# A state-space convolution block: stores, seeds and statistics reordered, the first gates computed in the head

## The chip, the cores and the metric

The kernel runs on one core of a Trainium2 chip. The metric is device time in microseconds (us), as the median of the runs shown. Engines are named as in the profile: PE (TensorE matmul), PEld (its weight loads), DVE (VectorE), ACT (ScalarE), POOL (GpSimd) and SP (SyncE, which issues nearly all DMAs here).

## What is computed

The input is `x` of 4 images, 128 channels, 96 x 96. It is normalised in 32 groups of channels, laid out as four sequences (rows forward and reversed, columns forward and reversed), put through one block with shared weights, and the four results are fused and added to `x`:

```python
def _scan1d(x, ...):                       # HID, MH, G, K = 256, 32, 4, 5
    t = _grouped1x1(x, in_proj_w, in_proj_b, G)
    u, gate = (t[:, :HID], t[:, HID:])
    u = silu(u)
    u = depthwise_conv(u, dw_w)            # 5 taps along the sequence
    s = _conv1x1(u, ssm_in_w)
    a = DMIN + (DMAX - DMIN) * sigmoid(_conv1x1(u, ssm_delta_w, ssm_delta_b))
    bb = tanh(_conv1x1(u, ssm_b_w, ssm_b_b))
    cc = tanh(_conv1x1(u, ssm_c_w, ssm_c_b))
    hst = <first-order recurrence h = a * h + bb * s along the sequence>
    u = u + _conv1x1(cc * hst + ssm_d[None, :, None] * s, ssm_out_w)
    u = _grouped1x1(u * sigmoid(gate), mix_w, mix_b, G)
    return _conv1x1(u, out_proj_w, out_proj_b)
...
return x + fuse(concat of the four directions)
```

## The kernel before

**Units, pairs, phases.** The work is cut into 8 phases: for each of the 4 images first the column order ("V"), then the row order ("H"). A phase has 6 steps of 4 pairs, so 24 pairs (`NP`), and there are 192 pairs in all. A pair `t` has two units `s` = 0 and 1, a forward and a reversed sequence, each of 384 positions with 256 channels in two halves `j`. A step's four pairs have the places `p` = 1, 2, 3, 0 (`TURN`); "offset" below is `t % 24`, and `k = t % 4`.

**Front and back.** In pair `t` the front works 4 pairs ahead: `front(t + 4)` does the input projection and SiLU of a quarter of a step (`compute_front`). Only steps 0 to 2 of a phase compute it ("fresh"); steps 3 to 5 are the same data met from the other end and load the SiLU stored before. A pair with a computed front is called fronted (offsets 20 to 23 and 0 to 7), the others unfronted. The pair's own convolution follows: half `j` = 1 by five taps on VectorE (`taps`, L765, the first tap on ScalarE, L763), half `j` = 0 by band matmuls on PE (`conv`). What the band lacks at the edge comes in two ways: places `p` = 1 and 2 add "less" matmuls (`conv_less`, which ends with a ScalarE copy of `u` out of PSUM, L736 or L738), places 3 and 0 ("single" pairs) add a row block on VectorE (`add_lone`, L717), from a tile that `keep_lone` stores to DRAM and `load_lone` brings back. `proj` computes `s`, `a`, `bb`, `cc` (PE, then ScalarE L802, L805, L810, then GpSimd L812, L813). `recurrence` runs the scan on VectorE (L839) in pairs with `k` < 2 and the outputs on GpSimd (L845 to L848). `scale_s` (L822) is the multiplication by `ssm_d`.

The back works `LAG` = 6 pairs behind, on pair `n = t - 6`: `under` (L560, ScalarE) seeds two PSUM banks with `u`, `out_of` (L548, PE) adds the state's output, `gating` (L664, VectorE) multiplies by the gate, and one pair later `accumulate` (PE, ScalarE L872 or L874, GpSimd L891) adds the mixed and fused product to the output held in SBUF.

**Gates.** The gate of pair `n` is four matmuls (`gate`, L528) and a tanh on ScalarE (L564, L570). The first 12 gates of a phase are computed, stored in DRAM (`kept`), and the second 12 load one of those, because they meet the same positions from the other end: `mirror(n)` gives offsets 12, 13, 14, 15 the gates 9, 8, 11, 10, and so on. There are two tiles for gates, `tile_of(n) = gates[n % 2]`. The gate of pair `n + 1` is computed in pair `n`; the gates of a phase's first three pairs are computed in pairs of offset 17 to 19, into the tile `shared`, and go through DRAM.

**Order.** `manual_schedule` takes each engine's order, SP's too, from the order in which the code issues. Waits follow from which tile or bank an instruction reads and writes. An instruction that waits holds all that stand behind it on its engine.

**Statistics.** While an image's V phase runs, the next image's input passes through three buffers, and VectorE takes `bn_stats` of 384 columns at a time (`stats_chunks`). In the H phase `stats_finish`, a generator, turns these into weights and biases, two steps of it in every pair with `k` > 1.

**Head.** Pairs 0 to 7 are issued by `pair`, the others by `pair_on`. Pairs 0 to 5 have no back. Pairs 6 and 7 have one, with their own gates computed in place; pair 8 computes two sets of gates (L1084 to L1095 and that of pair 9's `n`).

## Time and profile before

| | us |
|---|---|
| runs of before: median | 1783.57 |
| lowest, highest of 3 | 1782.19, 1784.2 |
| the profiled execution | 1788.7 |
| its span | 1787.0 |
| granted TensorE clock in it | 0.997 |

| group of instructions | count | busy us | mean ns |
|---|---|---|---|
| L765 DVE taps into PSUM | 576 | 589.0 | 1023 |
| L135 PE projection | 6144 | 538.2 | 491 |
| L135 PE mix and fuse | 6192 | 543.1 | 485 |
| L891 POOL add to the output | 375 | 411.2 | 1119 |
| L560 ACT seed | 380 | 298.2 | 799 |
| L738 and L736 ACT copy of u | 53 and 94 | 42.4 and 40.5 | 799 and 483 |
| L822 ACT scaling of s | 192 | 118.4 | 617 |

How to read it: the busy share of an engine is over the whole span; a group is one line of the code with one shape; a row of the timeline has its start, its duration, engine, line, operation, output and input, count, and in brackets the idle time ahead of it with what ended that. Matmuls overlap, four column groups at a time, so a mean duration of PE is no cost of one. PE works through its queue in order, and so do the other engines.

### The profile page before, as it was taken

The page shows a single profiled execution, that of the slowest core. Times are in us where ns is not written, and L with a number is a line of the kernel's source. Part 1 is how long each engine was busy: PE and PEld are TensorE (multiplying, and loading weights), DVE is VectorE, ACT ScalarE, POOL GpSimd, SP SyncE. Part 2 cuts the span into 40 slices and gives each one's busy share as a digit, 9 for nine tenths or more (in the row PEclk, how much of TensorE's full clock was granted, in tenths as well). Part 3 has the DMA queues.
Part 4 walks back from the last instruction along what each step waited for, and adds up shares of the span by engine and source line. Part 5 has one row for each costly group of instructions (what it writes and reads, how often), then busy time and mean ns, then how long its engine had stood idle before and what let it go on. Part 6 is the DMA issues. An engine that isn't in the chain of part 4 may idle for free.

```text
span 1787.0 us, 54377 instructions
## 1 busy us (share of the span) xinstructions
PE 1739.9 (97%) x22618; PEld 661.0 (37%) x22618; DVE 1496.9 (84%) x1526; ACT 1492.7 (84%) x2551; POOL 1423.3 (80%) x1477
## 2 busy tenths in 40 slices
PE   6999999999999999999999999999999999999998
PEld 3334333443334433344333443334433343334433
DVE  6888888887889888888778988888877888888887
ACT  4888888888888888888888888888888888888875
POOL 3578788877878878887777888888787888888886
PEclk9999999999999999999999999999999999999999
DMA  7775975558996688456798688744889749756464
GB/s 238 213 248 193 304 232 166 202 189 278 292 335 233 233 261 243 143 198 230 249 329 301 217 276 262 225 160 163 276 257 316 260 151 311 239 183 198 166 208 176
DMA packets 193814, 417.89 MB, mean 234 GB/s; under 512 B 17312, under 2 KB 154912, under 8 KB 193568
## 3 DMA queue, kind: packets, MB, share of 16 engines
q1 hardware_dynamic: 193424, 414.37, 70.5%
q8 instruction: 179, 2.93, 0.7%
q14 instruction: 67, 0.55, 0.1%
q10 hardware_dynamic: 144, 0.04, 0.0%
HBM read 250.58 MB, written 163.76 MB: 232 GB/s over the span
## 4 chain that ended last, share of the span: by engine, by line
PE 81%; DMA 8%; ACT 4%; DVE 3%; POOL 2%; issue 1%; SPq 1%; DVEq 0%; ACTq 0%; POOLq 0%
PE psum L135 68%; PE psum L548 8%; PE psum L528 5%; DMA kept<-shared 2%; DVE psum L765 1%; DMA x_in<-in_xs 1%; DMA out<-acc 1%; DMA lone<-edge 1%; ACT sil L498 1%; DMA edge<-sil 1%; ACT psum L560 1%; DVE u L664 1%; DMA xs<-in_xr 1%; ACT psum L763 1%; ACT shared L564 0%
## 5 line engine op out<-in xcount | busy, mean ns | idle before, releaser
L765 DVE SCALAR_TENSOR_TENSOR psum<-sil,small,psum 128x768 f32<-128x768 f32 x576 | 589.0, 1023 | 51.7 <-ACT psum L763 26.3
L135 PE MATMUL psum<-u,main 128*32 128x384 f32 x6144 | 538.2, 491 | 13.8 <-ACT shared L564 7.2
L135 PE MATMUL psum<-u,w_fin 128*32 128x384 f32 (+1 forms) x6192 | 543.1, 485 | 1.6 <-ACT ys L872 0.4
L664 DVE SCALAR_TENSOR_TENSOR u<-gate,psum 128x768 f32<-128x768 f32 x376 | 341.8, 950 | 181.2 <-PE psum L548 65.8
L891 POOL TENSOR_TENSOR acc<-ys,acc 128x384 f32<-128x384 f32 x375 | 411.2, 1119 | 21.2 <-ACT ys L874 4.5
L845 POOL TENSOR_TENSOR t<-t,t 64x384 f32<-64x384 f32 (+1 forms) x192 | 235.3, 1225 | 137.8 <-DVE t L839 84.3
L135 PEld LDWEIGHTS psum<-u,w_fin 128*32 128x32 f32 x6192 | 194.5, 110 | 313.0 <-issue 233.9
L135 PEld LDWEIGHTS psum<-u,main 128*32 128x32 f32 x6144 | 181.4, 110 | 342.6 <-issue 219.6
L560 ACT COPY psum<-u 128x768 f32<-128x768 f32 x380 | 298.2, 799 | 9.2 <-DVE u L664 4.4
L135 PE MATMUL psum<-sil,band 128*32 128x384 f32 x3072 | 285.5, 488 | 0.3 <-ACT gate L570 0.3
L846 POOL TENSOR_TENSOR t<-t,t 64x384 f32<-64x384 f32 (+1 forms) x192 | 272.3, 1418 | 15.1
L812 POOL TENSOR_SCALAR t<-tm 64x384 f32<-64x384 f32 x191 | 177.1, 927 | 110.3 <-ACT tm L802 84.0
L763 ACT ACTIVATE psum<-sil,small 128x768 f32<-128x768 f32 x191 | 172.5, 903 | 86.0 <-DVE u L664 83.6
L548 PE MATMUL psum<-t,main 32*128 32x384 f32 x1536 | 209.6, 524 | 4.5 <-ACT psum L560 3.3
L813 POOL TENSOR_TENSOR t<-t,tm 64x384 f32<-64x384 f32 x192 | 196.7, 1025 | 16.8 <-ACT t L805 1.6
L765 DVE SCALAR_TENSOR_TENSOR u<-sil,small,psum 128x768 f32<-128x768 f32 x192 | 194.9, 1015 | 6.9
L498 ACT ACTIVATE sil<-psum,bnorm 128x385 f32<-128x385 f32 x384 | 192.2, 584 | 3.9 <-PE psum L135 1.8
L528 PE MATMUL psum<-x_in,wn 32*128 32x384 f32 x768 | 167.9, 495 | 3.6 <-DVE shift L259 1.4
L135 PEld LDWEIGHTS psum<-sil,band 128*32 128x32 f32 x3072 | 89.8, 108 | 171.3 <-issue 60.6
L874 ACT COPY ys<-psum 128x384 f32<-128x384 f32 x281 | 129.5, 477 | 14.9 <-PE psum L135 11.8
L564 ACT ACTIVATE gate<-psum,bnorm 128x384 f32<-128x384 f32 x148 | 85.8, 581 | 57.1 <-PE psum L528 56.8
L802 ACT ACTIVATE tm<-psum,small 128x384 f32<-128x384 f32 x192 | 111.1, 579 | 11.6 <-PE psum L135 3.4
(105 smaller groups left out, 1512.0 us busy)
## 6 DMA issues: line engine op xcount, KB each, us to landing
sil<-sil SPq DMA_DIRECT2D x128, 770.0 KB, 6.5
gate<-kept SPq DMA_DIRECT2D x113, 768.0 KB, 6.2
kept<-gate SPq DMA_DIRECT2D x75, 768.0 KB, 3.6
lone<-edge SPq DMA_DIRECT2D x46, 770.0 KB, 7.3
x_in<-in_xs SPq DMA_DIRECT2D x194, 96.2 KB, 3.9
edge<-sil SPq DMA_DIRECT2D x96, 192.5 KB, 6.9
out<-acc SPq DMA_DIRECT2D x48, 384.0 KB, 7.9
kept<-shared SPq DMA_DIRECT2D x21, 768.0 KB, 5.2
```

What stands on the lines that cost most here:

```text
L135: nc.tensor.matmul(o[r, : rhs.shape[-1]], lhsT, rhs, start=start, stop=stop, skip_group_check=True)
L498: nc.scalar.activation(sils[step][:, s, j, g, :], bank(bk)[:, : N + 1], AF.Silu, bias=bn[:, 1:2] if j else bn[:, 4 + g : 5 + g],)
L528: nc.tensor.matmul(bank(to)[:, :N], stats[un["b"]][0][r, s, :], x_in[s][r, q, off : off + N], start=True, stop=True)
L548: nc.tensor.matmul(bank(ssm(bi, s) + j)[:, :N], w_so[r, bass.ts(j, P)], z[r, :], start=bi not in seeded, stop=True, skip_group_check=True)
L560: nc.scalar.copy(psum[:, ssm(bi, s) : ssm(bi, s) + 2, :N], us[bi][:, s])
L664: nc.vector.scalar_tensor_tensor(v, g, 1.0, pz, ALU.add, ALU.mult)
L763: nc.scalar.activation(part, src, AF.Copy, scale=w_tap[:, 0:1])
L765: nc.vector.scalar_tensor_tensor(us[i][:, :, 1, :] if k == K - 1 else part, src, w_tap[:, k : k + 1], part, ALU.mult, ALU.add,)
L813: nc.gpsimd.tensor_mul(ta[0:64, p, :], tb[0:64, :], tm[0:64, :])
L845: engine.tensor_mul(ta[0:64, p, r], tb[64:P, r], ta[64:P, p, r])
L846: engine.tensor_add(tb[0:64, r], ta[0:64, p, r], tb[0:64, r])
L891: adder.tensor_add(part, y, part)
```

## The change

It has seven parts.

1. **Head.** `pair` is used for pairs 0 to 5 only. In them VectorE copies `u` out of PSUM (two copies of 128 x 384) where ScalarE did, and GpSimd scales `s`. Each of these pairs also computes one unit of the gates of `n` = 0, 1, 2: two `gate` matmuls into banks 2 and 3, two tanh, a `load_gate`, and a store after the second unit; gates 0 and 1 also stay in their tiles, gate 2 goes through `shared`. Pairs 6, 7 and 8 become ordinary pairs of `pair_on`, without gates in 6 and 7, and pair 8 with one set.
2. **Seed.** In unfronted pairs that are not single, ScalarE's copy of `u` is issued behind `under(bi, 0)`.
3. **Gate tiles.** `tile_of` swaps the two tiles from each phase's middle on. Gates 10 and 11 of a phase aren't stored, and the pairs of offset 14 and 15 don't load one: they read what their tile holds, which is what pairs 12 and 13 loaded. The load for pair 12 is issued in pair 10 and goes to the tile in which the gate of pair 11 was computed.
4. **Edge rows.** `keep_lone` is issued in `after_front` as soon as the fourth quarter of a step has its SiLU; `load_lone` always in the step's first pair.
5. **Order on SP.** At a pair's end the chunk loads and the x loads for later gates are issued ahead of the gate store, no longer behind it.
6. **Statistics.** The generator becomes a table of small functions, each with an offset and one of three places in the pair; four small operations and the scaling of the weights move from VectorE to GpSimd. `stats_chunks` comes behind gating in pairs that are not single.
7. **Scaling at the turn.** At offset 19 `scale_s` is left out at the pair's end and done in pair 20, with that pair's own.

```diff
+    def stats_finish(b):
...
+        def spreads():
+            nc.vector.tensor_copy(mean, pm[:, 0:1])
+            nc.gpsimd.tensor_sub(dev, mv[:, 0:1], mean)
+            nc.gpsimd.tensor_mul(ex, dev, dev)
+            nc.gpsimd.tensor_add(ex, ex, mv[:, 1:2])
+            nc.gpsimd.tensor_scalar(gm4, gmask, mean, None, ALU.mult)
...
+        def guess():
+            bits = inv.bitcast(I32)
+            nc.vector.tensor_single_scalar(bits, var.bitcast(I32), 1, ALU.logical_shift_right)
+            nc.vector.tensor_scalar(bits, bits, -1.0, float(0x5F3759DF), ALU.mult, ALU.add)
+            newton()
...
+        def biases():
+            product(pm[:, 0:4], wn, gm4)
             for g in range(4):
                 for q in range(R):
+                    mm(pm[:, 4 + g : 5 + g], q, wn[0:32, 32 * g : 32 * g + 32], mean[0:32, :], True, True)
...
+        return {
+            (0, 0): gather,
+            (1, 1): means,
+            (1, 2): spreads,
+            (2, 1): variances,
+            (2, 2): lambda: nc.vector.tensor_scalar_add(var, pm[:, 0:2], GN_EPS),
+            (3, 0): guess,
+            (4, 0): newton,
+            (5, 0): newton,
+            (6, 0): scale_w,
+            (7, 1): biases,
+            (7, 2): finish,
+        }
...
+        if g == R - 1 and fresh(step):
+            keep_lone(step)
...
     def tile_of(n):
-        return gates[n % 2]
+        return gates[(n + (n + NP // 2) // NP) % 2]
+
+    def stays(m):
+        return NP // 2 - 3 < m < NP // 2
 
     def load_kept(n):
         m = mirror(n)
-        if n % NP < 3 and NP <= n < NU // 2:
+        if n % NP < 3 and 1 < n < NU // 2:
             nc.sync.dma_start(tile_of(n), kept[n // NP % 2][n % NP])
-        if n < NU // 2 - R and m is not None:
+        if n < NU // 2 - R and m is not None and not stays(m):
             nc.sync.dma_start(tile_of(n), kept[n // NP % 2][m])
...
     def pair(t):
...
+        i = 2 * t
+        banks = head_banks(t)
+        if t == R:
+            load_lone(1)
         if t:
             new_u(i)
             taps(i, range(1, K))
             conv(i, banks)
+            conv_less(i, banks, False)
+            for s in range(2):
+                nc.vector.tensor_copy(us[i][:, s, 0, :], bank(min(banks) + s)[:, :N])
             first_tap(i + 2)
             front(t + R, FRONT if banks == PROJ else (5, 4, 2, 3))
         recurrence(t)
         stats_chunks(t)
...
+        if t == 2:
+            keep_lone(0)
+        load_chunks(t + 2)
+        proj(i, banks)
+        n, s = divmod(t, 2)
+        if s == 0:
+            early[0] = tile_of(n) if n < 2 else shared()[:, : 4 * N].rearrange(
+                "p (s j n) -> p s j n", s=2, j=2
+            )
+        for j in range(2):
+            gate(2 * n, s, j, 2 + j)
+        for j in range(2):
+            tanh_one(n, early[0], s, j, 2 + j)
+        load_gate(2 * n + s + UB)
+        if s:
+            nc.sync.dma_start(kept[0][n], early[0])
+        if t > 0:
+            s = tbs[i - 2][0:64, :]
+            nc.gpsimd.tensor_scalar(s, s, d_sb[0:64, 0:1], None, ALU.mult)
 
     def pair_on(t):
...
-        if k == (1 if fresh(un["step"]) else 0):
+        if k == 0:
             load_lone(un["step"])
...
         if not fronted:
             if not single:
-                conv_less(i, banks)
+                conv_less(i, banks, False)
             under(bi, 0)
...
+            if not single:
+                copy_u(i, banks)
+        add_next(w[1])
         if fronted:
             if not single:
                 conv_less(i, banks)
+            if t % NP == 20:
+                scale_s(i - 4)
             scale_s(i - 2)
...
+        piece(t, 2)
+        if not single:
+            stats_chunks(t)
         first_tap(i + 2)
         if gated is not None:
             tanh_both(gated, to, 0, 6)
-            nc.sync.dma_start(kept[gated // NP % 2][gated % NP], to)
...
+        if t + 2 < end:
+            load_chunks(t + 2)
+        if gated is not None:
             for s in range(2):
                 load_gate(2 * gated + s + UB)
...
+        if gated is not None and not stays(gated % NP):
+            nc.sync.dma_start(kept[gated // NP % 2][gated % NP], to)
...
-        if not fronted:
+        if not fronted and (t % NP != 19 or t + R >= end):
             scale_s(i - 2)
...
         start()
-        for t in range(LAG + 2):
+        for t in range(LAG):
             pair(t)
-        for t in range(LAG + 2, NU // 2):
+        for t in range(LAG, NU // 2):
             pair_on(t)
         tail()
```

More of the change, by code (lines that the diff above doesn't have):

```diff
@@ L733, in conv_less, with copy_u @@
                    False, True)
+        if copy:
+            copy_u(i, banks)
+    def copy_u(i, banks):
+        b0 = min(banks)
         if banks == PROJ:
@@ L896, in accumulate, with piece @@
         return add
-    later, soon = [], []
+    later, soon = {}, []
+    def piece(t, place):
+        later.pop((t % NP, place), lambda: None)()
     waiting, held = [], []
@@ L958, in pair @@
         recurrence(t)
-        un = units[i]
         stats_chunks(t)
-        if t % R == 2 and t < LAG + 2:
-            keep_lone(un["step"])
-        ending = old and t % (2 * NP) > NP + NP // 2
-        def stats_piece(at_end=False):
-            if later and k > 1 and at_end == ending and t % (2 * NP) not in (27, 39):
-                next(later[0], None)
-        if not ahead:
-            free[0] = w[1]
-            stats_piece()
-        if seed and with_front:
-            for s in (1, 0):
-                under(bi, s)
@@ L976, in pair @@
-        for add in held:
-            add()
-        held.clear()
-        if waiting:
-            add = accumulate(waiting.pop(0), w[0], *final)
-            if late:
-                held.append(add)
-            else:
-                add()
-        between = ahead and not old
-        if between:
-            conv_less(i, banks)
-        if seed and not with_front:
-            under(bi, 0)
-        if ahead:
-            accumulate(waiting.pop(0), w[1], *final)()
-            free[0] = w[0]
-            stats_piece()
-            if not between:
-                conv_less(i, banks)
```

261 lines of the change are left out of this document (54 added, 207 removed).

## The prediction

> **What bounds the kernel now.** I read the page first, then the waits, then each engine's timeline for single pairs. The page's first part:
>
> ```profile
> PE 1739.9 (97%) x22618; PEld 661.0 (37%) x22618; DVE 1496.9 (84%) x1526; ACT 1492.7 (84%) x2551; POOL 1423.3 (80%) x1477
> ```
>
> TensorE is busy 97% of the span, so only what PE itself executes or waits for can move the end. The change leaves PE's matmuls almost as they are; the question is where PE stands still or runs slower than its rhythm. One `tm` activation (L802) runs per pair, so the distance of two of them on ScalarE is the length of a pair. ScalarE's timeline (start, duration):
>
> ```profile
> 38.52 0.58 ACT L802 ACTIVATE tm<-psum,small 128x384 f32<-128x384 f32 x1
> ...
> 69.95 0.59 ACT L802 ACTIVATE tm<-psum,small 128x384 f32<-128x384 f32 x1
> ...
> 103.25 0.58 ACT L802 ACTIVATE tm<-psum,small 128x384 f32<-128x384 f32 x1
> ...
> 112.67 0.58 ACT L802 ACTIVATE tm<-psum,small 128x384 f32<-128x384 f32 x1
> ...
> 1130.02 0.58 ACT L802 ACTIVATE tm<-psum,small 128x384 f32<-128x384 f32 x1
> ...
> 1138.55 0.58 ACT L802 ACTIVATE tm<-psum,small 128x384 f32<-128x384 f32 x1
> ...
> 1149.56 0.56 ACT L802 ACTIVATE tm<-psum,small 128x384 f32<-128x384 f32 x1
> ```
>
> Pairs 1 to 5 take 31.4 us together and pairs 6 to 8 take 33.3; pair 9 takes 9.42, pair 122 takes 8.53, and pair 123, which differs from 122 in nothing but a piece of statistics, 11.01. Pairs of one kind repeat to a hundredth except where something is late. The waits that reach PE (engine and line, released by, total us, times, longest):
>
> ```profile
> DVE u L717 <- DMA lone<-edge: 5.6, 2, 3.0
> ...
> ACT shared L564 <- DMA kept<-shared: 10.8, 8, 3.1
> ...
> PE psum L135 <- ACT shared L564: 7.2, 9, 2.6
> ...
> PE psum L135 <- DVE u L717: 4.2, 3, 1.8
> ```
>
> A late edge transfer and a late store of gates each stop PE a few times. These, the statistics, the head, and one short wait in every second unfronted pair are what the change touches.
>
> **The change, part by part.** I give each part as what it does to PE; minus is time saved.
>
> *Seed ahead of the u copy.* In an unfronted pair that is not single (offsets 8, 9, 12, 13, 16, 17 of each 24), ScalarE copies `u` (L738) and then seeds the output banks (`under`, L560). Pair 37 is such a pair, pair 10 is a single one, without that copy:
>
> ```profile
> 361.00 0.58 ACT L872 ACTIVATE ys<-psum,b_fin 128x384 f32<-128x384 f32 x1 [0.17 <-PE psum L135]
> 361.84 0.80 ACT L738 COPY u<-psum 128x768 f32<-128x768 f32 x1 [0.26 <-PE psum L135]
> 362.54 0.81 ACT L560 COPY psum<-u 128x768 f32<-128x768 f32 x1
> ...
> 363.09 0.58 PE L528 MATMUL psum<-x_in,wn 32*128 32x384 f32 x1
> 363.49 0.60 PE L548 MATMUL psum<-t,main 32*128 32x384 f32 x3
> ...
> 117.01 0.58 PE L528 MATMUL psum<-x_in,wn 32*128 32x384 f32 x1
> 117.18 0.60 PE L548 MATMUL psum<-t,main 32*128 32x384 f32 x3
> ```
>
> The first output product comes 0.40 after the gate's product here and 0.17 in the single pair; the seed ends at 363.35, just ahead of 363.49. Seeding first, it would start at 361.6 (after `ys`) and end at 362.4, before PE gets there. That is 0.23 a pair, in 6 x 8 pairs less pair 8, which I count in the head: 47. I take 0.2, **-9.4**; bounds 0 and -10.8. The copy of `u` then ends at 363.2, where the seed ends now; its readers are the projection at the pair's end, and bank 7's gate, which stands behind three output products. If that cover is gone, the saving goes with it.
>
> *Statistics.* PE's, VectorE's and ScalarE's timelines in pair 27 (the same pair as 123, two images earlier), and the same operation in the head:
>
> ```profile
> 271.82 0.24 PE L135 MATMUL psum<-mv,gmean 128*32 128x1 f32 x8 [0.31 <-ACT ys L874]
> ...
> 272.93 1.26 DVE L202 SCALAR_TENSOR_TENSOR ex<-dev,mv 128x1 f32<-128x1 f32 x1
> 274.11 1.25 DVE L204 TENSOR_SCALAR gm<-gmask,mean 128x4 f32<-128x4 f32 x1
> ...
> 276.25 0.91 ACT L763 ACTIVATE psum<-sil,small 128x768 f32<-128x768 f32 x1 [3.60 <-DVE u L664]
> ...
> 20.82 0.22 DVE L202 SCALAR_TENSOR_TENSOR ex<-dev,mv 128x1 f32<-128x1 f32 x1
> ```
>
> Two one-column operations of 1.25 stand in VectorE's row ahead of gating, ScalarE's next tap waits 3.60, and the pair is 11.01 - 8.53 = 2.5 too long. After the change `dev`, `ex` and `gm4` run on GpSimd, whose adds and outputs have a pair's slack, and the rest comes behind gating. Three images: -7.5. Added: the bias product is 40 short matmuls instead of 16, at 0.24/8 = 0.03 each 0.7 a time, +2.1. Sum **-5.4**; bounds -7.5 and 0 (the wait only moves).
>
> Why is the same operation 0.22 in the head and 1.26 here? GpSimd is idle there and adding here. [...]
>
> *Edge rows.* `keep_lone` moves one pair earlier, behind the last SiLU of its step, and `load_lone` from the step's second pair to its first: same four stores and one load, 9 us earlier. On SP they now stand behind the x loads and ahead of reloads, chunks and kept gates; SP may wait for the edge stores there, but nothing behind it is due in that pair. The waits above (PE 4.2, DVE 5.6) go: **-5**; bounds 0 and -5.6.
>
> *Gate stores.* Two stores and two loads of 768 KB fall away per phase (gates 10 and 11; pairs 14 and 15), the others are issued behind the chunk and x loads. The stalls at offsets 18 and 19 come from stores on a full queue (SP's timeline; then engines' busy time, clock, DMA share and GB/s in one 2 us stretch):
>
> ```profile
> 191.90 0.34 SPq L1143 DMA_DIRECT2D kept<-shared  x1
> 192.34 2.09 SPq L299 DMA_DIRECT2D x_in<-in_xs  x2
> ...
> 184.00:186.00 2.00, 2.00 (x28) 0.78 (x24) 1.93 (x3) 1.94 (x4) 1.87 (x2) 1.00 1.09 402
> ```
>
> Gone transfers empty the queue by 768 KB at 402 GB/s, some 2 us each, ahead of these stores; but the store now stands behind up to 2.09 us of issuing. I take half of PE's 7.2: **-3.5**; bounds -7.2 and +7 (1 us at each of seven phases).
>
> *Scaling at the turn.* At offset 19 `scale_s` leaves the place ahead of the next pair's SiLUs:
>
> ```profile
> 204.75 0.62 ACT L822 ACTIVATE t<-t,small 64x384 f32<-64x384 f32 x1
> 205.39 2.00 ACT L498 ACTIVATE sil<-psum,bnorm 128x385 f32<-128x385 f32 x4
> ```
>
> The accumulation waits for those SiLUs' banks, so up to 0.62 in seven phases; 0.5 each, **-3.5**, bounds 0 and -4.3. It is made up for in pair 20 behind the u copies, where ScalarE waits for gating anyway.
>
> *The head.* VectorE's row in pair 4, its chunk wait in pair 2, a PSUM operand of 384 columns on VectorE, and eight gate matmuls:
>
> ```profile
> 60.78 1.75 DVE L839 TENSOR_TENSOR_SCAN t<-t 64x768 f32<-64x768 f32 x1
> 62.57 0.56 DVE L412 BATCH_NORM_STATS2 bn<-xs 128x6 f32<-128x384 f32 x1
> 63.05 3.12 DVE L765 SCALAR_TENSOR_TENSOR psum<-sil,small,psum 128x768 f32<-128x768 f32 x3
> 66.20 1.01 DVE L765 SCALAR_TENSOR_TENSOR u<-sil,small,psum 128x768 f32<-128x768 f32 x1
> ...
> 50.08 0.56 DVE L412 BATCH_NORM_STATS2 bn<-xs 128x6 f32<-128x384 f32 x1 [2.98 <-DMA xs<-in_xr]
> ...
> L891 DVE TENSOR_TENSOR acc<-psum,acc 128x384 f32<-128x384 f32 x5 | 2.7, 545 | 0.0
> ...
> 74.64 1.50 PE L528 MATMUL psum<-x_in,wn 32*128 32x384 f32 x8
> ```
>
> The copy of `u` from PSUM on VectorE isn't in the trace; the nearest row is the add of 545 ns. It could be hidden (0) or held by GpSimd like L202 (1 us more each, ten copies, +10). I take 0.55. VectorE in pairs 1 to 5 then has five times 4.13 of taps and 1.1 of copies, 0.56 in four pairs, a scan in two: 32. The chunk wait keeps its end, so the copies of pairs 1 and 2 fill 2.2 of its 2.98; 0.8 stays, and pair 1 is led by PE, about 1 more: 33.8 against 31.4, **+2.4**. ScalarE loses copies and scaling and gets two tanh; PE gets two gates a pair (0.4), hidden while VectorE leads. GpSimd, nearly idle there, takes the scaling. SP gets six x loads and three stores earlier, behind the chunks. Pairs 6 to 8 lose twelve gates and their waits, and 6 and 7 take edge rows on VectorE in place of the less products: pair 6 has no accumulation and is led by taps, seed, gating and next tap, some 9.6; 7 as 8.53, 8 as 9.42: 27.5 against 33.3, -5.8. Head **-3**, bounds -8 and +10.
>
> *Gates of pair 11.* `tile_of` now gives pair 12 the tile that holds gate 11, and `load_kept(12)` stands in pair 10 ahead of the gating of pair 11, which must then wait for that load:
>
> ```profile
> 173.20 0.89 ACT L570 ACTIVATE gate<-psum,bnorm 128x768 f32<-128x768 f32 x1
> ...
> 180.70 1.82 DVE L664 SCALAR_TENSOR_TENSOR u<-gate,psum 128x768 f32<-128x768 f32 x2 [0.76 <-PE psum L548]
> ...
> gate<-kept SPq DMA_DIRECT2D x113, 768.0 KB, 6.2
> ...
> DMA to landing us min/median/max: 3.2/5.1/11.5
> ```
>
> The load can start at 174.1 (after the tanh), gating wants it at 180.7: 6.6 later, against a median of 6.2 and, for that tile, 11.5 at most. **+2** over eight phases; bounds 0 and +33 (below).
>
> **Sum**: -9.4 - 5.4 - 5 - 3.5 - 3.5 - 3 + 2 = -27.8. The profiled execution took 1788.7 (span 1787.0), 5.1 above the median of 1783.57; 1788.7 - 27.8 = 1760.9 there, **1756** as a median.
>
> **Rivals.**
> - *All stalls go* (14%): 10.8 + 7.5 + 5.6 + 7.2 + 4.3 + 6 = 41.4 saved: 1742. For it: PE is otherwise in rhythm. Against: a store still stands behind loads.
> - *The seed buys nothing* (12%), because `ys` or the taps end late and hold it: 9.4 less, 1765. Against: taps end 361.3, as the seed's free slot begins.
> - *Stores come later than before* (9%): -3.5 becomes +7, 1766. For: DMA share 1.09.
> - *VectorE's copies are held in the head* (5%): ten more, 1766.
> - *Slower: gating of pair 11 waits for its tile's load* (10%). If that load takes the 11.5 of the slowest, it lands 4.9 after gating wants it, less the 0.76 VectorE idles there: 4.1 x 8 = 33 instead of 2, 1787. It costs from 7.4 on, and outweighs the rest from about 11.1. Against: two stores fewer stand ahead of it.
> - The forecast itself: 50%.
>
> Measurement tells about 0.2%, 3.6 us, from no change. The slower rival's upper half lies within or above that: slower 8%, same 2%, faster 90%. The range 1738 to 1778 leaves out the slower rival and the ends beyond the two bounds.
>
> **What would show it.** Pairs 9, 12, 13 at 9.2 instead of 9.42, output products 0.17 behind the gate; pair 27 below 9; no L717 wait on the edge load; less wait of the tanh into `shared` on its store; pairs 1 to 5 near 34 and pair 8 near 9.4; VectorE's gating in pair 17, 41 and so on waiting for a DMA of at most 1 us. The prediction fails if that last wait is several us, or if the unfronted pairs keep their 9.42.

## The result, and the profile after

| | before | after |
|---|---|---|
| median of 6 runs each, us | 1784.41 | 1777.17 |
| lowest, highest | 1782.19, 1790.21 | 1771.6, 1777.8 |
| profiled execution, its span | 1788.7, 1787.0 | 1777.6, 1775.9 |

The ratio of the times is 0.9942, with a 95% interval of 0.992 to 0.9964: a gain of 0.6%, small but clear of no change, 7 us where 28 were forecast. The profile after answers first with its busy times, then with the waits that the prediction had shown (engine, line and what released it; total us, times, longest):

```profile
PE 1731.3 (97%) x22658; PEld 645.6 (36%) x22658; DVE 1483.8 (84%) x1510; ACT 1488.2 (84%) x2537; POOL 1446.2 (81%) x1500
```

```profile
DVE u L633 <- DMA gate<-kept: 20.9, 13, 3.7
...
ACT shared L582 <- DMA kept<-shared: 14.8, 9, 2.6
DVE t L813 <- POOL t L787: 14.5, 9, 2.1
...
PE psum L130 <- ACT shared L582: 9.7, 9, 1.9
```

The wait for the edge rows is gone from the list. In its place stand two that were absent or nearly so before, VectorE's gating (L633) waiting for a kept gate and VectorE's scan (L813) waiting for GpSimd, and the wait for the gate stores has grown from 10.8 to 14.8. The pairs' ends, from ScalarE's timeline of after (pairs 0, 5, 8 and 9; L776 was L802):

```profile
42.92 0.60 ACT L776 ACTIVATE tm<-psum,small 128x384 f32<-128x384 f32 x1
...
76.99 0.58 ACT L776 ACTIVATE tm<-psum,small 128x384 f32<-128x384 f32 x1
...
104.57 0.57 ACT L776 ACTIVATE tm<-psum,small 128x384 f32<-128x384 f32 x1
...
113.43 0.58 ACT L776 ACTIVATE tm<-psum,small 128x384 f32<-128x384 f32 x1
```

Two things can be read off. The head costs what was forecast: pairs 1 to 5 take 34.1 (31.4 before), pairs 6 to 8 27.6 (33.3). And the first `tm` starts 4.4 us later than before, in a stretch that the change doesn't touch. The windows of after say why; the columns behind each engine's busy time are the granted clock, the DMA share and GB/s:

```profile
25.00:30.00 5.00, 5.00 (x88) 2.10 (x72) 0.35 (x6) 3.92 (x8) 0.00 (x0) 0.50 0.05 16
30.00:35.00 5.00, 5.00 (x38) 3.71 (x32) 1.14 (x2) 2.19 (x5) 1.97 (x3) 0.50 0.40 102
```

The same 10 us in the profile of before:

```profile
25.00:30.00 5.00, 5.00 (x104) 3.51 (x88) 0.91 (x6) 4.49 (x10) 0.51 (x1) 1.00 0.40 107
30.00:35.00 5.00, 5.00 (x90) 2.08 (x95) 4.41 (x10) 3.79 (x8) 2.65 (x4) 1.00 0.31 80
```

The granted clock was 0.50 against 1.00. In ten of the twelve runs below, whose start is the same code, the first `tm` came at 37.5 to 38.8, and in two (e2, e5) at 41.9 and 43.2: it belongs to an execution and not to the change. So kernels are compared below from pair 0 to pair 191: 1716.8 us before, 1701.1 after, **-15.7**. The medians differ by 7.2 only. Of the rest, 4.4 went at the start, and the profiled execution of before lies 4.3 above its median, that of after 0.4 above its own. Whether those 4.3 lie in the pairs no run shows, so the gain of 15.7 may be some us too large.

The length of a pair is the distance of two `tm`. After minus before, summed over the phases by offset (pairs 9 to 191, from ScalarE's timelines; what isn't listed adds up to within 0.1):

| offset | us | what is in it |
|---|---|---|
| 2, 3 | -5.3, -7.9 | stalls of edge rows and of the statistics gone |
| 9, 13, 16, 17 | -3.5, -3.2, -3.0, -2.4 | seed ahead of the u copy |
| 20, 21 | -4.1, -0.6 | scaling at the turn |
| 1, 5, 6, 15 | -1.9, -2.3, -1.6, -1.1 | shorter behind a pair that grew, or rid of statistics (6, 15) |
| 0, 4 | +2.5, +8.0 | gating waits for a kept gate (at offset 4 of phases 1, 3, 5 the scan waits for GpSimd too, 1.0 to 1.3) |
| 8, 12 | +3.4, +2.6 | scan waits for GpSimd |
| 18 | +5.3 | tanh waits for the gate store |
| 7, 10 | +1.7, +0.9 | bias product in phases 1, 3, 5; a pair behind the seeded one (+0.5 in e7 too) |

Gains of 36.9 stand against losses of 24.4; with the head's -3.1 this makes the -15.7. The gains are the forecast's; the losses are three new stalls. Each shows in the timelines of after. **Gate store**, pair 18 (SP's rows, then ScalarE's and PE's):

```profile
183.38 2.58 SPq L315 DMA_DIRECT2D x_in<-in_xs  x4
186.08 0.51 SPq L1030 DMA_DIRECT2D kept<-shared  x1
...
190.83 1.05 ACT L582 ACTIVATE shared<-psum,bnorm 128x384 f32<-128x384 f32 x2 [2.59 <-DMA kept<-shared]
...
191.47 4.48 PE L130 MATMUL psum<-u,main 128*32 128x384 f32 x32 [1.92 <-ACT shared L582]
```

The store stands behind four x loads whose issuing takes 2.58, and the next tanh into `shared` may not write until the store has read it. **Kept gate**, pair 100 (SP's rows, then VectorE's):

```profile
920.68 2.61 SPq L671 DMA_DIRECT2D edge<-sil  x4
923.40 0.58 SPq L493 DMA_DIRECT2D sil<-sil  x1
924.08 1.06 SPq L609 DMA_DIRECT2D gate<-kept  x1
...
933.57 1.82 DVE L633 SCALAR_TENSOR_TENSOR u<-gate,psum 128x768 f32<-128x768 f32 x2 [3.66 <-DMA gate<-kept]
```

In pairs with `k` = 3 the load of a kept gate is one deferred from the pair ahead (`soon`). The edge stores, now issued inside `front`, stand ahead of it. **Scan**, pair 60 (GpSimd's rows, then VectorE's):

```profile
564.31 2.43 POOL L865 TENSOR_TENSOR acc<-ys,acc 128x384 f32<-128x384 f32 x2
566.83 0.94 POOL L786 TENSOR_SCALAR t<-tm 64x384 f32<-64x384 f32 x1
567.85 1.01 POOL L787 TENSOR_TENSOR t<-t,tm 64x384 f32<-64x384 f32 x1
...
568.89 2.86 DVE L813 TENSOR_TENSOR_SCAN t<-t,t 64x768 f32<-64x768 f32 x1 [2.12 <-POOL t L787]
```

GpSimd has no gap here; the product that the scan needs stands behind two additions, and the scan, with the gating behind it, is 2.12 late.

### The profile page after: what moved, and what is told of

Same layout as the page of the kernel before. It is cut to its first block, busy times and chain, and to the rows that moved or that the text cites. A ratio compares the mean times of both kernels' runs of the same rounds, so it can differ in the third digit from the quotient of the medians.

```text
span 1775.9 us, 54441 instructions
## 1 busy us (share of the span) xinstructions
PE 1731.3 (97%) x22658; PEld 645.6 (36%) x22658; DVE 1483.8 (84%) x1510; ACT 1488.2 (84%) x2537; POOL 1446.2 (81%) x1500
## 4 chain that ended last, share of the span: by engine, by line
PE 84%; DMA 4%; POOL 4%; ACT 3%; DVE 3%; issue 2%; SPq 0%; POOLq 0%; DVEq 0%; ACTq 0%
PE psum L130 72%; PE psum L566 7%; PE psum L546 5%; DMA kept<-shared 3%; DMA gate<-kept 1%; POOL acc L865 1%; DVE u L633 1%; POOL t L819 1%; DVE psum L739 1%; POOL t L787 1%; POOL t L820 1%; ACT psum L737 1%; ACT shared L582 0%; DMA acc<-in_xr 0%; POOL t L786 0%
## 5 line engine op out<-in xcount | busy, mean ns | idle before, releaser
L633 DVE SCALAR_TENSOR_TENSOR u<-gate,psum 128x768 f32<-128x768 f32 x376 | 341.8, 950 | 189.2 <-PE psum L566 68.6
L865 POOL TENSOR_TENSOR acc<-ys,acc 128x384 f32<-128x384 f32 x375 | 410.9, 1119 | 20.9 <-DMA acc<-in_xr 3.6
L819 POOL TENSOR_TENSOR t<-t,t 64x384 f32<-64x384 f32 (+1 forms) x192 | 244.6, 1274 | 127.9 <-DVE t L813 105.1
L820 POOL TENSOR_TENSOR t<-t,t 64x384 f32<-64x384 f32 (+1 forms) x192 | 271.9, 1416 | 15.1
L786 POOL TENSOR_SCALAR t<-tm 64x384 f32<-64x384 f32 x191 | 181.2, 949 | 88.2 <-ACT tm L776 68.1
L566 PE MATMUL psum<-t,main 32*128 32x384 f32 x1536 | 225.1, 525 | 4.3 <-ACT psum L578 4.2
L516 ACT ACTIVATE sil<-psum,bnorm 128x385 f32<-128x385 f32 x384 | 192.4, 584 | 11.2 <-PE psum L130 8.4
L546 PE MATMUL psum<-x_in,wn 32*128 32x384 f32 x768 | 160.7, 496 | 0.0
L848 ACT COPY ys<-psum 128x384 f32<-128x384 f32 x281 | 129.2, 477 | 20.9 <-PE psum L130 18.1
L776 ACT ACTIVATE tm<-psum,small 128x384 f32<-128x384 f32 x192 | 111.0, 578 | 13.2 <-PE psum L130 5.7
```

Source lines behind the costliest of these rows:

```text
L516: nc.scalar.activation(sils[step][:, s, j, g, :], bank(bk)[:, : N + 1], AF.Silu, bias=bn[:, 1:2] if j else bn[:, 4 + g : 5 + g],)
L546: nc.tensor.matmul(bank(to)[:, :N], stats[un["b"]][0][r, s, :], x_in[s][r, q, off : off + N], start=True, stop=True)
L566: nc.tensor.matmul(bank(ssm(bi, s) + j)[:, :N], w_so[r, bass.ts(j, P)], z[r, :], start=bi not in seeded, stop=True, skip_group_check=True)
L633: nc.vector.scalar_tensor_tensor(v, g, 1.0, pz, ALU.add, ALU.mult)
L819: engine.tensor_mul(ta[0:64, p, r], tb[64:P, r], ta[64:P, p, r])
L820: engine.tensor_add(tb[0:64, r], ta[0:64, p, r], tb[0:64, r])
```

## The experiments

One execution each, except e8 and e12. "Pairs" is the time from the `tm` of pair 0 to that of pair 191: 1716.8 before, 1701.1 after. Where transfers decide (offsets 0, 4, 13, 19, and pair 4 of the head) single pairs differ by 1 to 2 us from one execution to the next, so I take a sum of pairs as good to some 3 us (an estimate, with one profiled execution of each kernel); pairs in which nothing is late repeat to 0.02.

| run | kernel | us | before, same chip | pairs |
|---|---|---|---|---|
| e1 | after, deferred load ahead of the front | 1774.03 | 1788.73 | 1702.5 |
| e2 | after, gate store behind its tanh | 1774.57 | 1788.73 | 1699.0 |
| e3 | after, tiles and transfers as before | 1778.39 | 1788.73 | 1707.3 |
| e4 | after, ScalarE copies and scales in the head | 1776.86 | 1788.73 | 1704.7 |
| e5 | after, edge stores behind the deferred load | 1780.92 | 1793.48 | 1704.2 |
| e6 | after, additions of every fourth pair held | 1772.3 | 1793.48 | 1701.1 |
| e7 | before, seed alone | 1777.46 | 1793.48 | 1705.4 |
| e8 | after with e2, e5 and e6 | 1763.86 | 1793.48 | 1692.9 |
| e9 | before, edge rows alone | 1786.23 | 1782.48 | 1714.7 |
| e10 | after, seed as before | 1784.77 | 1782.48 | 1713.0 |
| e11 | after, weights scaled on VectorE | 1772.52 | 1782.48 | 1700.3 |
| e12 | e8 with e11 | 1754.62 | 1788.4 | 1680.6 |

### Seed: e7 and e10

e7 makes only this edit in the kernel before:

```diff
-    def conv_less(i, banks):
+    def conv_less(i, banks, copy=True):
...
             if not single:
-                conv_less(i, banks)
+                conv_less(i, banks, False)
             under(bi, 0)
+            if not single:
+                copy_u(i, banks)
```

> The kernel before with one edit of the change alone: in the pairs without a front the seed of the state products goes ahead of ScalarE's copy of u. The prediction put it at 0.2 us a pair at offsets 9, 12, 13, 16, 17, -9.4 us in all. Reading of the changed kernel's trace: 0.3 to 0.45 us a pair, so pairs of offset 9, 13, 16 and 17 go from 9.42 to 9.0 to 9.1, -13 to -18 us without losses. If GpSimd's backlog is brought by the shorter pairs alone, offset 12 in phases 2, 4 and 6 rises from 9.42 to about 10.9 here too; if it is brought by the statistics that moved to GpSimd, it falls to 9.05 in all phases. tm(0) to tm(191) then 1701 to 1704 with the backlog, 1697 to 1700 without it, against 1716.8.

Pairs 1705.4, **-11.4**. Offsets 9, 13, 16 and 17 fall by 3.0, 3.3, 3.0 and 2.6, 0.3 to 0.55 a pair. Offset 12 falls from 9.42 to 9.05 in the phases 0, 1, 3, 5 and 7 and stays at 9.48 to 9.52 in 2, 4 and 6, far from after's 10.7 to 11.1: the seed brings a little of GpSimd's lateness there, but not most of it. e10 undoes the edit in the kernel after.

> The changed kernel with the seed behind ScalarE's copy of u again, as in the kernel before. It tells which of two makes GpSimd late at offsets 8 and 12: shorter pairs, or statistics moved to GpSimd. By shorter pairs: the scan's waits for GpSimd's product at offset 12 go (9.42 in all phases, against 10.7 to 11.1 in phases 2, 4, 6), and offset 8 in odd phases falls from 11.1 toward 10. By the statistics: offset 8 in odd phases stays at 11.1. The other offsets (9, 13, 16, 17) return to 9.42; tm(0) to tm(191) about 1708 if the seed's net gain in the change is some 7 us, 1712 if it is the 11.4 us of e7_seed_alone.

Pairs 1713.0, so in the changed kernel the seed is worth 11.9. Offset 12 stays at 10.84, 11.51 and 10.06 in phases 2, 4, 6, and offset 8 at 10.6 to 11.5 in odd ones: the pairs that the seed shortens aren't what makes GpSimd late at either place.

### Edge rows: e9, e1 and e5

e9 moves the edge rows in the kernel before and nothing else:

```diff
     def after_front(step, g):
...
+        if g == R - 1 and fresh(step):
+            keep_lone(step)
...
-        if k == 0 and fresh(un["step"]):
-            keep_lone(un["step"])
-        if k == (1 if fresh(un["step"]) else 0):
+        if k == 0:
             load_lone(un["step"])
```

> The kernel before with the edge-row step of the change alone: the four stores right behind the last SiLU of their step, the load in the step's first pair. Prediction: the stalls of the lone rows at offset 2 go, about -5 us, and nothing else moves. Reading of the changed kernel: offset 2 falls by about 5 us over the phases (9.96, 11.64, 9.61 to 8.52), but the deferred gate load stands behind the stores and pairs of offsets 0 and 4 wait for it, some +2 and +4 us; in all tm(0) to tm(191) within 2 us of the 1716.8 before. If the loss at offset 4 comes instead from the shorter pairs ahead of it (statistics gone from offset 3), it does not appear here and the run is near 1712.

Pairs 1714.7, -2.1, about what was expected, but less than a sum is good to, and in device time the one run of e9 is 3.75 above the one of before on its chip. At offset 2 5.7 is gained, at offsets 0 and 4 3.0 and 8.9 are lost. So the loss at offset 4 comes from the edge rows themselves. Two more changes weren't expected. Offset 12 in phases 2, 4 and 6 rises to 10.70, 10.67 and 10.15, with the seed and the statistics as before. And offset 3 falls by 5.4 in the phases with statistics, whose code is untouched. Pair 27 of e9 (VectorE's rows, then GpSimd's):

```profile
272.33 0.52 DVE L202 SCALAR_TENSOR_TENSOR ex<-dev,mv 128x1 f32<-128x1 f32 x1
272.77 0.22 DVE L204 TENSOR_SCALAR gm<-gmask,mean 128x4 f32<-128x4 f32 x1
...
271.09 1.18 POOL L848 TENSOR_TENSOR t<-t,t 64x384 f32<-64x384 f32 x1
272.34 0.50 POOL L850 COPY t<-t 64x384 f32<-64x384 f32 x1
272.92 1.23 POOL L893 TENSOR_TENSOR acc<-ys,acc 128x384 f32<-128x384 f32 x1
```

The two operations that took 1.26 and 1.25 in the prediction's rows take 0.52 and 0.22: the pair runs some 0.6 earlier against GpSimd, and beside them stand a copy of 0.50 and the gap behind it, where two additions of 1.19 stood.

The traces put the cause of offset 12 four pairs ahead. Phases 2, 4 and 6 begin an image, and in pair 56 (offset 8 of phase 2) GpSimd adds to an accumulator that was loaded just before. SP's rows and GpSimd's, first before, then e9:

```profile
523.79 2.67 SPq L1075 DMA_DIRECT2D acc<-in_xr  x4
527.74 3.03 SPq L702 DMA_DIRECT2D edge<-sil  x4
...
536.39 4.76 POOL L891 TENSOR_TENSOR acc<-ys,acc 128x384 f32<-128x384 f32 x4
...
521.51 3.79 SPq L704 DMA_DIRECT2D edge<-sil  x4
526.25 3.56 SPq L1075 DMA_DIRECT2D acc<-in_xr  x4
...
536.28 4.75 POOL L893 TENSOR_TENSOR acc<-ys,acc 128x384 f32<-128x384 f32 x4 [1.85 <-DMA acc<-in_xr]
```

The edge stores, a pair earlier, now stand ahead of this load too, and GpSimd waits 1.85, 1.86 and 1.48 for it at offset 8 of phases 2, 4 and 6. From there to pair 60 it has no more gap, and there the scan waits for it (1.23, 1.19 and 1.13 in the three phases). In before and e7, where the edge stores stand behind the load, GpSimd's additions at offset 8 don't wait for a transfer; in every run with the early stores they do, at offset 8 or 9, by 0.8 to 3.6.

e1 and e5 keep the edge rows early and put the deferred load of the kept gate ahead of them, in e1 ahead of the whole front, in e5 behind the front's x loads (first e1, then e5):

```diff
-        front(t + R, FRONT)
         for e in soon:
             load_kept(e)
         soon.clear()
+        front(t + R, FRONT)
```

```diff
     def after_front(step, g):
...
-        if g == R - 1 and fresh(step):
-            keep_lone(step)
...
             front(t + R, FRONT if banks == PROJ else (5, 4, 2, 3))
+            if t % R == R - 1:
+                keep_lone(t // R + 1)
...
         soon.clear()
+        if fronted and g == R - 1:
+            keep_lone(step)
```

> The changed kernel, with one thing moved: in a pair with k = 3 the deferred load of kept gates is issued ahead of the front, and so ahead of the four edge stores of keep_lone. Theory (the edge stores hold the gate load on SP): the gating waits on a kept gate at offsets 0 and 4 (13 waits, 20.9 us in all) go to under 3 us, pairs of offset 4 in phases 2 and 4 come back from 11.81 and 11.35 to about 9.4, pairs of offset 0 from 9.4-10.0 to about 9.35; sum 6 to 8 us less than the changed kernel. Rival (the queue itself is full, the order is no matter): these pairs keep their length within 0.3 us. Offsets 8, 12 and 18 stay as they are by both.

> The four stores of edge rows go behind the deferred load of a kept gate instead of ahead of it; everything else as in the changed kernel. Theory: the waits of the gating for its kept gate at offsets 0 and 4 (13 of them, 20.9 us in all) come from those stores standing ahead of the load on SP. Expected: they fall to the single 1.00 at pair 17, pairs of offset 0 go back from about 9.7 to 9.33, pairs of offset 4 in odd phases likewise, and phases 2 and 4 do not rise to 13.1 and 13.4 as in e1_kept_first, because the x loads of the front stay ahead of the deferred load: tm(0) to tm(191) 1695 to 1699 us against 1701.1. Rival (the queue is full anyway, whatever its order): the wait moves to the load of the edge rows or to x_in and the pairs keep their length within 1 us a phase, 1701.

The waits for a kept gate fall from 20.9 to 1.0 and 3.1, pairs of offset 0 to 9.33, and those of offset 4 in phases 1, 3 and 5 to 9.3 to 9.7: the order on SP was the cause of that wait. The sum doesn't follow. Offsets 1 and 5, which had been shorter behind a long pair, give 2.1 back each, and offset 4 in phases 2 and 4 takes 13.1 and 13.4 in e1, 11.6 and 13.6 in e5, where after has 11.8 and 11.4. Pair 4, in the head, takes 8.4 in e1 and 10.5 in e5, against 6.9 in after. In these pairs TensorE waits for the front's x loads, in e1:

```profile
487.92 2.05 PE L130 MATMUL psum<-x_in,wn 32*32 32x385 f32 x32 [1.74 <-DMA x_in<-in_xs]
```

So e1's expectation held for the wait and not for the time, and e5's first theory fell for phases 2 and 4: the x loads are late there whichever side the gate load stands on. Part of that is what e5's rival said, a wait that moves to `x_in`.

### Gate stores and tiles: e2 and e3

e2 issues the store of a gate straight behind the tanh that fills its tile, ahead of the chunk and x loads:

```diff
             tanh_both(gated, to, 0, 6)
+            if not stays(gated % NP):
+                nc.sync.dma_start(kept[gated // NP % 2][gated % NP], to)
...
-        if gated is not None and not stays(gated % NP):
-            nc.sync.dma_start(kept[gated // NP % 2][gated % NP], to)
```

> The changed kernel, with the gate store issued again straight behind the last tanh, ahead of the chunk and x loads. Theory (the store behind up to four x loads comes 2.5 us later): pairs of offset 18 in phases 0, 2 and 4 come from 10.29, 9.96 and 9.84 to 8.3-8.5, the tanh's wait on the store (14.8 us, 9 times) falls below 5 us; 5 to 6 us less than the changed kernel at offsets 18 and 19. Rival (DMA volume sets when the store lands): offset 18 falls by less than 0.5 us and the stall comes back at offset 19, as before the change (10.96, 9.97).

Offset 18 falls by 4.7, to 8.4 or 8.5 in the phases 0, 2 and 4 where it had been long, and offset 19 by 3.2. The wait for the stores, in e2's list of waits:

```profile
ACT shared L582 <- DMA kept<-shared: 4.9, 4, 2.3
```

Against 10.8 before and 14.8 after: this is the place of the new stall. Offset 17 takes 1.5 more and the head 1.6, and offsets 0 and 4 differ by 0.9 and 1.3 as they do from one execution to the next; 2.1 is left of the sum. e3 takes the other half of the edit back, the tiles and the transfers left out:

```diff
     def tile_of(n):
-        return gates[(n + (n + NP // 2) // NP) % 2]
+        return gates[n % 2]

     def stays(m):
-        return NP // 2 - 3 < m < NP // 2
+        return False
```

> The changed kernel with the gates' tiles and transfers as before: tile n % 2, all twelve gates stored, all twelve loaded, so that pairs 11, 14 and 15 of a phase read their own gates and not those that pairs 12 and 13 load. Theory of the prediction (two stores and two loads fewer empty the queue): offsets 18 and 19 get longer by 1 to 2 us in the phases with chunks, 3 to 6 us in all; the wait of pair 17's gating (1.00 us once) goes. Rival (these transfers were hidden): the total stays within 1.5 us of the changed kernel's pairs.

Pairs 1707.3, +6.1. Offset 18 takes 3.7 more, in phases 0, 2 and 4, and offsets 19 and 20 give 1.7 and 1.2 of that back; the rest is mostly in single pairs at offsets 0, 4 and 13 and in pair 4 (1.1 to 1.7 each) that wait for transfers and vary. So the total is beyond the rival's 1.5, but at the pairs that wait for the stores the transfers left out are worth between 1 and 4 us by this one execution, and the order of the store, which stands in the same pairs, loses 4.7 at offset 18.

### GpSimd: e6 and e11

e6 lets the two additions of each pair with `k` = 3 wait for the next pair, where they stand behind GpSimd's product and outputs:

```diff
-                held.append(add) if late else add()
+                held.append(add) if late or (k == R - 1 and t + R < end) else add()
```

> In the last pair of each group of four GpSimd's two additions into the accumulator are issued one pair later, behind that pair's outputs; nothing is added or left out. Theory: the scan's waits for GpSimd's recurrence product (9 waits, 14.5 us) come from GpSimd's queue being as long as the shorter pairs, with 2.4 us of additions ahead of the product. Expected: these waits vanish, pairs of offset 8 in odd phases fall from 11.1 to about 9.5 and pairs of offset 12 in phases 2, 4 and 6 from 10.9 to about 9.05, some 10 to 12 us in all: tm(0) to tm(191) about 1690. Rival (GpSimd's 7.8 us of work a pair is a bound over the whole stretch): the time comes back as later outputs, that is as waits of TensorE at the output products one or two pairs on, and the total stays within 3 us of 1701.

e6's list of waits has one left of the nine:

```profile
DVE t L813 <- POOL t L787: 1.0, 1, 1.0
```

Offset 8 falls by 5.5 (9.09, 9.50 and 9.08 in phases 1, 3, 5) and offset 12 by 4.8. The sum of pairs is unchanged in this execution, 1701.1: offset 4 took 4.3 more and offset 0 2.1 more, with more waits for kept gates (25.6 in all, against 20.9) and for x loads (3.8, against 0.3), and the head 1.4 more. The order theory holds for the waits. The rival's sum came, but not by its way: what TensorE itself waits at the output products is 4.2 in e6 as in after. e8 and e12, where the kept gates' wait is gone as well, decide it. e11 puts one piece of the statistics, the scaling of the input weights, back on VectorE. On GpSimd in after (least, median and largest duration in ns):

```profile
L260 POOL TENSOR_SCALAR wn<-main,inv x6: 602/604/613, 303.9 to 1171.5; 128x128 f32<-128x128 f32 x6
```

The edit:

```diff
         def scale_w():
             for e in range(2):
-                nc.gpsimd.tensor_scalar(wns[:, e, :], w_in[:, e, :], inv[:, e : e + 1], None, ALU.mult)
+                nc.vector.tensor_scalar_mul(wns[:, e, :], w_in[:, e, :], inv[:, e : e + 1])
```

> The changed kernel with the two scalings of the input weights (128x128 each, 1.20 us on GpSimd, place 6 of the statistics) on VectorE again. If GpSimd's 2.4 us there are what its product is late by at offset 8, pairs of offset 8 in odd phases fall from 11.1 to about 9.6 and the rest stays: -4 to -5 us, tm(0) to tm(191) about 1696. If the lateness is one of all shorter pairs, they fall by less than 0.5 each, and VectorE's scalings lengthen offset 6 by up to 0.5.

The expectation took the 1.20 of the two for that of one; they take 1.2 together, and offset 8 in odd phases falls by just that, 1.17, 1.09 and 1.14, to 9.94, 9.79 and 9.91. Offset 6 stays at 8.53; offset 12 in phases 2, 4, 6 doesn't fall (11.2, 12.2, 11.2). So offset 8 is late mainly by the weights' scaling, and offset 12 is not. The sum misses the expected 1696: 1700.3, because offsets 0, 4 and 12 took 1.8 to 2.1 more each in this execution.

### The head: e4

```diff
-            conv_less(i, banks, False)
-            for s in range(2):
-                nc.vector.tensor_copy(us[i][:, s, 0, :], bank(min(banks) + s)[:, :N])
+            conv_less(i, banks)
...
-            s = tbs[i - 2][0:64, :]
-            nc.gpsimd.tensor_scalar(s, s, d_sb[0:64, 0:1], None, ALU.mult)
+            scale_s(i - 2)
```

> The changed kernel, with ScalarE copying u and scaling s again in pairs 1 to 5. In the changed kernel these pairs take 34.1 us together (31.4 before). Theory of the prediction (VectorE leads there: 32 us of its own work): without the copies VectorE has 5.5 us less, and pairs 1 to 5 take 31.5 to 32.5. Rival (ScalarE leads once it has two tanh more): copies 0.8, first tap 0.9, four SiLUs 2.0, tm, t and tanh 1.6, scaling 0.6, two gates' tanh 1.1 make 7.0 a pair, 35 us.

```profile
38.62 0.58 ACT L776 ACTIVATE tm<-psum,small 128x384 f32<-128x384 f32 x1
...
73.35 0.61 ACT L776 ACTIVATE tm<-psum,small 128x384 f32<-128x384 f32 x1
```

Pairs 0 and 5 of e4: 34.7 for five pairs, against 34.1 in after and 34.1 to 35.5 in the other runs with after's head that keep the edge rows' place. VectorE is relieved of 1.1 a pair and the pairs don't get shorter, so VectorE's copies alone aren't what made them longer, and taking them off ScalarE buys nothing that shows. The traces name a third engine. What TensorE waits in pairs 1 to 5, before and after, and its gate matmuls of one such pair in after:

```profile
PE psum L135 <- DVE u L765: 2.4, 4, 1.2
...
PE psum L130 <- DVE u L904: 0.3, 1, 0.3
...
56.75 0.91 PE L546 MATMUL psum<-x_in,wn 32*128 32x384 f32 x4
```

By the profile TensorE is busy 33.8 of the 34.1 in after, and in e4 it has no wait at all there, while VectorE is busy 29.3 in after and ScalarE 32.2 of 34.7 in e4. The gates cost 0.91 a pair, 4.6 in five, and the 2.4 of waiting is gone: that is about the difference. No run leaves these gates out, so this is read from the traces and not shown by an edit.

### All repairs: e8 and e12

e8 joins e2, e5 and e6; e12 adds e11.

> The changed kernel with three orders repaired together: edge rows behind the deferred gate load, the gate store straight behind the tanh that fills the tile, GpSimd's additions of every fourth pair held for a pair. If the three causes are separate their gains add: about -4 (offsets 0 and 4), -5 (offset 18) and -10 (offsets 8 and 12) from 1777, so 1758 us (ratio to before 0.985). If they share one limit (the next engine is close behind), the sum comes back in other pairs and it stays at 1770 or above.

> e8_all_three with the two scalings of the input weights on VectorE again (e11_scale_dve). In e8 pairs of offset 8 in odd phases still took 10.04 us against 9.54 in even ones. If what is left there is GpSimd's 2.4 us of scalings, they fall to about 9.5, -1.6 in all, and tm(0) to tm(191) goes from 1692.9 to about 1691; the ratio to before stays near 0.983 (0.979 to 0.986). If VectorE's two scalings hold up a gating at offset 6, those pairs lengthen from 8.52 by up to 0.5 and the sum is unchanged.

e8 has a ratio to before of 0.9834 (0.9797 to 0.9871), e12 of **0.9819 (0.9794 to 0.9844)**; neither interval meets after's 0.992 to 0.9964, each measured against before on its own chip, so both beat both kernels. The expected 0.985 of e8 lies within its interval, but not by gains that simply add: offsets 0, 8, 12, 18 and 19 are 19.6 shorter than in after, and 8.3 is left of the sum. e12's 12.3 on top is far more than the 1.6 expected. In e12 the offsets 0 (9.3 to 9.5), 8 (9.1 in odd phases), 12 (9.0 to 9.1) and 18 (8.3 to 8.5) are all in rhythm, but for the last phase. Its waits:

```profile
ACT shared L580 <- DMA kept<-shared: 6.0, 5, 2.2
...
DVE u L631 <- DMA gate<-kept: 1.2, 1, 1.2
...
PE psum L130 <- DMA x_in<-in_xs: 0.5, 1, 0.5
```

The scan's wait for GpSimd is gone and that for a kept gate has one case left, in pair 17. Pairs are 20.6 shorter than after's. Of the 12.3 between e8 and e12, 2.8 lie at offset 8, where the edit is, another 6.5 at offset 4 in phases 2 and 4 (13.28 and 13.59 in e8, 10.03 and 10.39 in e12) and 2.6 in pair 4. TensorE's wait for the x loads in these three pairs, 1.5 to 2.2 each in e8, is 0.5 in pair 4 of e12 and absent in the other two. The two ran on different chips; whether the chip or VectorE's scaling took that wait away stays open.

## Why the prediction was wrong

Most mechanisms were the right ones, the sum was not: three steps took for free what wasn't, and the head came out right by luck.

- **Edge rows (-5).** The step that failed is "nothing behind it is due in that pair": behind the four stores on SP stood the kept gate deferred from the pair ahead. The 5.3 at offset 2 came as forecast, and 10.5 went at offsets 0 and 4, of which offsets 1 and 5 gave 4.1 back. Alone the move is worth 2.1, and without the statistics' gain of 5.4 that it carries it loses. The loads of the accumulators stood behind the stores as well; by e9's trace that is where the 2.6 at offset 12 comes from.
- **Gate stores (-3.5).** Half of PE's 7.2 was to go; the rival "stores come later than before" (9%) happened instead. PE's wait grew to 9.7 and offset 18 to +5.3. The step that failed is the size of the delay: the transfers left out were worth 1 to 4 at offsets 18 to 20 (e3), but the store's place behind 2.58 of issuing cost 4.7 and 3.2 at offsets 18 and 19 (e2).
- **Statistics (-5.4).** The step that failed is that GpSimd's "adds and outputs have a pair's slack". What was taken off VectorE came off (pair 27 takes 8.53; offset 3 -7.9), the bias product cost 1.7 where 2.1 stood, but the scan needs GpSimd's product in the pair after `k` = 3, and with 1.2 of weights' scaling ahead of it, it came late at offset 8 in three phases, 1.3 to 1.6 each. Also, the small operations took 1.26 and 1.25 beside additions of 1.19, and 0.52 and 0.22 beside a copy of 0.50 and a gap in e9, where the edge rows alone collect 5.4 of the gain. The two terms were added as if they were independent.
- **Seed (-9.4).** Right, and too small: 11.4 alone. In pair 37 of after the output product stands 0.01 behind the gate's, as the seed has ended long before it (ScalarE's rows, then PE's):

```profile
360.95 0.80 ACT L578 COPY psum<-u 128x768 f32<-128x768 f32 x1
361.68 0.80 ACT L712 COPY u<-psum 128x768 f32<-128x768 f32 x1
...
362.57 0.58 PE L546 MATMUL psum<-x_in,wn 32*128 32x384 f32 x1
362.58 0.60 PE L566 MATMUL psum<-t,main 32*128 32x384 f32 x3
```

  The prediction took 0.23, the distance to the single pair's 0.17, as the most there was; of the 0.40 nearly all, 0.39, went.
- **Scaling at the turn (-3.5).** Offset 20 gives -4.1. Offset 20 is fed by stores and loads as well (e9, which leaves the scaling alone, has -1.4 there), so some 2.7 to 4.1 is the scaling's; no run tests it alone.
- **The head (-3).** -3.1, with both halves as forecast (+2.6 and -5.7), the first by luck: the same head takes 34.1 to 35.5 in the other runs, and the reason given, that VectorE leads and hides PE's gates, is not what the traces show. Each pair has four gate matmuls in the profile, not two; they take 0.91 where 0.4 stood, and TensorE fills the pairs.
- **Gates of pair 11 (+2), and the slower rival.** In after the gating waits for that load once, 1.0 in pair 17, and offset 17 is 2.4 shorter. In phases 0 to 6 that load landed 4.1 to 4.7 after its issue; the rival's 11.5 never came.
- **Clock.** The profiled execution of after starts 4.4 us late, with a granted clock of 0.50 where before had 1.00, which the prediction couldn't know of. Whether the other five runs behind the median carry it too stays open.

The two operations of `guess` stay on VectorE. They took 0.33 and 0.17 in pair 27, the first ending as GpSimd's product of 1.03 ends. In pair 75 the second took 1.14, beside a product of 1.20:

```profile
271.52 0.33 DVE L254 TENSOR_SCALAR inv<-var 128x2 int32<-128x2 int32 x1
271.88 0.17 DVE L255 TENSOR_SCALAR inv<-inv 128x2 int32<-128x2 int32 x1
...
270.79 1.03 POOL L787 TENSOR_TENSOR t<-t,tm 64x384 f32<-64x384 f32 x1
...
705.78 1.14 DVE L255 TENSOR_SCALAR inv<-inv 128x2 int32<-128x2 int32 x1
...
705.70 1.20 POOL L819 TENSOR_TENSOR t<-t,t 64x384 f32<-64x384 f32 x1
```

The longer one arose once in three images (pair 123 has 0.33 and 0.17 again), and pair 75 takes 8.53 like pair 27: VectorE still waits 0.36 for TensorE ahead of its gating there, against 1.16 in pair 27, so the time came out of its idle time.

What is shown: the place of each of the three stalls, by an edit that takes it away (e2, e5, e6), and that with all three edits the kernel takes 0.9834 of before's time (e8), with the weights' scaling back on VectorE 0.9819 (e12). That e12's 1754.62 lies next to the forecast's 1756 confirms nothing: it is another kernel on another chip. What is read from traces and not shown by an edit: that GpSimd is late at offset 12 because the accumulators' load stands behind the edge stores (in e12 the additions at offset 8 still wait 1.3 to 2.0 for a transfer; holding two others back only keeps the scan from paying for it), and that TensorE leads in the head. What stays open: the x loads at offset 4 of phases 2 and 4.

## What to carry to other kernels

When a transfer is issued earlier, list what it is now ahead of in the issuing queue, deferred loads included, and when each of those is due; a wait that disappears at the transfer's own reader can return at theirs (here 5.6 us of waits at the edge rows went, and 20.9 for kept gates came). When the bound engine's rhythm gets shorter, recount the engines with "slack" per group of pairs and look at the order inside their queues: holding two additions back for a pair took away eight of nine waits. Look for the cause of a late engine further back than the pair that shows it: GpSimd's lateness at offset 12 began with a load four pairs earlier. Where a gain rests on how small operations of VectorE and GpSimd happen to meet, test each part alone before summing: at offset 3, where after gains 7.9, e9 gained 5.4 without the statistics' edit.

## What the runs showed of the hardware

Starts of the same code differed by 3 to 6 us. In the three of the fourteen profiled executions of this study that started late, the granted clock from 25 to 30 and from 30 to 35 us was 0.50 and 0.50 (after), 0.64 and 0.67 (e2), 0.57 and 0.50 (e5); in before, e6 and e8 it was 1.00 in both. In after it stood at 0.50 for 13 us, from 22 to 35, with TensorE busy all that time by the profile (5.00 of 5.00 in both windows shown above). What set it off, and what ended it, no run here shows.

One VectorE operation on 128 x 1 (`ex`, L202) took 0.22 us in the head of before with no GpSimd instruction beside it, 0.52 in pair 27 of e9 beside a copy of 0.50, and 1.26 in pair 27 of before beside an addition of 1.19. That GpSimd's instruction is what makes the difference is read from these rows and not shown by an edit.
